# A four-layer image network on one core: a convolution folded with the projection before it, and a normalisation on another engine

## The chip, the cores and the metric

The kernel runs on one core of a Trainium2 chip. A core has a matrix engine (TensorE, PE in the profile; its weight loads are listed apart as PEld), three engines for elementwise work (VectorE or DVE, ScalarE or ACT, GpSimd or POOL) and SyncE (SP), whose queue issues all the DMAs of this kernel. The engines run side by side, each in the order of its own queue. The metric is the device time of one execution in microseconds.

## The reference

The input is two images of 96 channels and 96 x 96 pixels, in float32. Each of four layers adds to its input a block that works on the group-normalised input: x = x + layer(gn(x)). All four blocks hold selective scans, recurrences h = a * h + b over 192 channels with 16 states each. Layer 0, the only one whose work changes, begins like this (`_gn` has 32 groups of three channels and no weights):

```python
xz = in_proj(gn(x))                # 96 -> 384 channels; the halves are xp and z
t  = conv3x3(xp, off1_w) + off1_b  # 192 -> 192 channels, zero padding
t  = gelu(batch_norm(t))
f  = tanh(off2(t))                 # 192 -> 2 channels: an offset for each pixel
xs = xp sampled bilinearly at the places that f gives
```

The sampled `xs` is then scanned in windows of 6 x 6 pixels in four directions. The four results are added, normalised over the channels, multiplied with silu(z) and projected back to 96 channels.

## The kernel before

Layer 0 is the class `Windows`, on a `Machine` whose tiles are T = 288 pixels wide. The layers 1, 2 and 3 run after it on a second machine (T = 384) as one common stretch, the trunk.

*Strips, jobs and steps.* Layer 0 cuts the two images into 32 strips of six rows (576 pixels). A strip has eight jobs: four directions by two halves of 288 pixels. A job has eight steps, and each step scans a group of channels and states as 128 partitions by 864 values. So a strip is 64 steps, and the layer 2048. `Machine.scan` walks over the steps n and writes out, in this order, what each engine gets at step n:

- PE: every second step `four_B` (into the tile `pb`, one for two steps), and `sum_states` of step n-2 (six products of the trace, into `py`).
- ACT: `decay` for step n+1, three activations into `dA`, and then whatever was put in the slot with `self.act` in the step before.
- DVE: the product `pd` of the loaded `w` with `pb`, and the scan `hs` of `dA` and `pd`.
- What the generators in flight have for this step: the next job's preamble (the products `wx` and `dtw`, the copy `p`, the two activations `v`, softplus), and the background jobs in `bg`.
- POOL: `hC`, the product of `hs` with the loaded `C`, which `sum_states` reads two steps later.

*The order is set by the program.* The class `Engine` chains all the instructions of an engine in the order in which the program issues them. It also issues them on one line of the file, which is why nearly every row of the profile names L156. Rows are told apart by their tiles.

*Sampling a strip.* `samples` is the generator that prepares the next strip while the present one is scanned. A `yield` ends what it does in a step. It starts with the preamble of a strip's first job, which runs ten steps ahead, so at step 6 of job 6 of the strip before:

1. It loads eight rows of the input (the strip and a row above and below) into `x8`, and on DVE `apply_gn` subtracts the group's mean and multiplies by its inverse deviation: the group `x<-x,gn`.
2. `in_proj`, four products with `w_in`, copied by ACT into `xp`, which has two halves of 96 channels, eight rows and 98 columns. The columns at the sides stay zero.
3. The convolution: for each half of the output channels and each half of the strip, 18 products (two halves of the input by nine taps) add up in a bank of PSUM, `po`. Four or three stand in each step, so it spans 20 steps. ACT copies each `po` with scale and bias of the batch norm into `t`.
4. Gelu on `t`, four pairs of products with `off2`, tanh into `f`, then some 18 products and sums on POOL that sample `xp` (tiles `top` and `t`).

*Ending a strip.* When a strip's last job is done, `ending` runs as a background generator beside the first jobs of the next strip: `channel_norm` on `yn` (products with a matrix of means into `pm` and `pb`, Ln and Exp on ACT), the normalisation of the strip's own input on DVE (`xn<-x,gn`), the projection of `z` in four products, silu, `w_out`, and the residual sum `o` on DVE. The method `bank` keeps apart the users of the only PSUM bank `pm`: in `Windows`, steps 7, 0 and 1 of a job belong to the preamble.

*Functions that share an ACT table.* An `ACT_TABLE_LOAD` stands in ACT's queue wherever the next function needs other tables: around softplus, gelu, silu, and for Ln and Exp.

*Weights.* `pack` brings the weights into the shapes of the loads, on the host. Before the change, `off1` is one load of 96 x 2 x 9 x 192 values.

Of the kernel before, what the change touches and what calls it, by code (L numbers as in the profile page):

```python
# [33 lines left out]
F32 = mybir.dt.float32  # L34
AF = mybir.ActivationFunctionType
ALU = mybir.AluOpType
# [4 lines left out]
B, C, S, L = 2, 96, 96, 96 * 96  # L41
# [34 lines left out]
def pack(i):  # L76
    i = {k: np.asarray(v) for k, v in i.items()}
    a = {"x": i["x"].reshape(B, C, L)}

    sel = np.zeros((32 + N, 4, 32, 4), np.float32)  # L80
    for q in range(4):
        for n in range(4):
            sel[32 + 4 * q + n, q, :, n] = 1
    a["sel"] = sel.reshape(32 + N, 512)
    a["zs"] = np.repeat(np.eye(32, dtype=np.float32), 4, 0)
    eye = np.eye(96, dtype=np.float32)
    gn = np.kron(np.eye(32), np.ones((3, 3))).astype(np.float32) / np.float32(3)
    one = np.ones((96, 96), np.float32)
    a["mats"] = np.stack([gn, one / np.float32(96), one / np.float32(192), eye, eye[::-1]], 1)

    q = lambda n: i[f"L0_conv_{n}"]
    a["L0_in"] = q("in_proj_w").T
    a["L0_out"] = _lhsT(q("out_proj_w"))
    off = q("off1_w").transpose(1, 2, 3, 0).reshape(2, 96, 9, 192)
    a["L0_off1"] = off.transpose(1, 0, 2, 3)
    off2 = _lhsT(q("off2_w").reshape(2, 192))
    a["L0_off2"] = np.broadcast_to(off2[..., None], (96, 2, 2, 96))
    a["L0_cols"] = _cols(
        q("off1_b"), q("bn_gamma"), q("bn_beta"), q("bn_mean"), q("bn_var"), q("ln_gamma"), q("ln_beta")
    )  # L100
    a |= _scan_weights(
        "L0", q("x_proj_weight"), q("dt_projs_weight"), q("dt_projs_bias"),
        q("A_logs").reshape(4, 192, N), q("Ds").reshape(4, 192),
    )

    q = lambda n: i[f"L1_conv_{n}"]
    a["L1_in"] = q("in_proj_w").T
    a["L1_out"] = _lhsT(q("out_proj_w"))


    w, taps = q("in_proj_w").T[:, :192], q("conv_w").reshape(192, 4)
    a["L1_in3"] = np.stack([np.concatenate([w, w[32 * t : 32 * t + 32]]) for t in range(3)], 1)
    a["L1_taps"] = np.repeat(np.stack([taps[:, :3].T, np.stack([taps[:, 3]] * 3)]), (96, 32), axis=0)
    a["L1_cols"] = _cols(q("conv_b"))
    a["L1_norm"] = np.stack([q("norm_g"), q("norm_b")], 1)
    a["L1_g1"] = q("gate_w1").T
    a["L1_g1b"] = q("gate_b1").reshape(24, 1)
    a["L1_g2"] = q("gate_w2").T
    a["L1_g2b"] = q("gate_b2").reshape(1, 4)
    a |= _scan_weights(  # L120
        "L1", q("x_proj_w")[None], q("dt_proj_w")[None], q("dt_proj_b")[None], q("A_log")[None], q("D")[None]
    )

    q = lambda n: i[f"L2_conv_{n}"]
    a["L2_in"] = q("in_proj_w").T
    a["L2_out"] = _lhsT(q("out_proj_w"))
    a["L2_taps"] = np.broadcast_to(q("conv_w").reshape(192, 9).T, (96, 9, 192))
    a["L2_cols"] = _cols(q("conv_b"), q("gn_gamma"), q("gn_beta"))
    a |= _scan_weights(
        "L2", q("x_proj_w"), q("dt_w"), q("dt_b"), q("A_logs").reshape(4, 192, N), q("Ds").reshape(4, 192)  # L130
    )

    q = lambda n: i[f"L3_conv_{n}"]
    a["L3_in"] = q("in_proj_w")
    a["L3_out"] = _lhsT(q("out_proj_w").T)
    a["L3_taps"] = np.broadcast_to(q("conv_w").reshape(192, 9).T, (96, 9, 192))
    a["L3_cols"] = _cols(q("conv_b"), q("ln_gamma"), q("ln_beta"))
    a |= _scan_weights(
        "L3", q("x_proj_weight").transpose(0, 2, 1), q("dt_proj_weight"), q("dt_proj_bias"),
        q("A_log")[None], q("D_skip")[None],  # L140
    )
    return {k: np.ascontiguousarray(v) for k, v in a.items()}
# [396 lines left out]
class Layer:  # L539
# [81 lines left out]
        return (yield from self.averaged(mv, self.const["gn"], 1e-5, f"gn{self.n}"))  # L621

    def apply_gn(self, out, x, gn):
        self.nc.vector.tensor_scalar(out, x, gn[:, 0:1], gn[:, 1:2], ALU.subtract, ALU.mult)

    def channel_norm(self, x, mat, sq):

# [22 lines left out]
    def ending(self, y, src, dst, stats, sz=None, xn=None, norm=None, gamma=None, beta=None):  # L650


        nc, hs = self.nc, range(2)
        size = y.shape[-1]
        sb = lambda tag, *shape, bufs=1: self.sb.tile([96, *shape], F32, tag=tag, name=tag, bufs=bufs)
        if sz is None:
            x, n = sb("x", size, bufs=3), sb("xn", size, bufs=3)
            nc.sync.dma_start(x, src)
            yield
        if norm is not None:  # L660
            yield from self.channel_norm(y, norm, sb("sq", 2, size))
        if sz is None:
            xn(n, x)
        else:
            x, z = sb("x", size, bufs=2), sb("z", 2, size, bufs=2)
            nc.sync.dma_start(z, sz)
            nc.sync.dma_start(x, src)
        if gamma is not None:
            for h in hs:
                self.act(  # L670
                    lambda h=h: nc.scalar.activation(
                        y[:, h, :], y[:, h, :], AF.Identity, scale=gamma(h), bias=beta(h)
                    )
                )
        yield
        if sz is None:
            z = sb("z", 2, size)
            for h in hs:
                for at in self.pieces(size):
                    yield from self.bank()  # L680
                    m = self.mm(self.ps()[:, : self.T], [(self.w_in[:, 192 + 96 * h : 288 + 96 * h], n[:, at])])
                    self.act(lambda h=h, at=at, m=m: nc.scalar.copy(z[:, h, at], m))
                    yield
            self.act(lambda: nc.scalar.activation(z, z, AF.Silu))
            yield
        yield
        for h in hs:
            nc.gpsimd.tensor_mul(y[:, h, :], y[:, h, :], z[:, h, :])
            yield
        o = sb("o", size, bufs=2)  # L690
        for i, at in enumerate(self.pieces(size)):
            yield from self.bank(2)
            m = self.mm(self.ps()[:, : self.T], [(self.w_out[:, h, :], y[:, h, at]) for h in hs])
            yield
            nc.vector.tensor_add(o[:, at], x[:, at], m)
            if stats is not None:
                nc.vector.bn_stats(stats[:, i, :], o[:, at])
            yield
        nc.sync.dma_start(dst, o)


class Windows(Layer):
# [9 lines left out]
    def load_weights(self):  # L712
        super().load_weights()
        nc = self.nc
        self.off1, self.off2 = self.load("off1"), self.load("off2")

        self.bn = self.w.tile([96, 2, 2], F32, tag="bn", name="bn")
        v = lambda i: self.cols[:, 2 * i : 2 * i + 2]
        s, b = self.bn[:, 0, :], self.bn[:, 1, :]
# [6 lines left out]
    def samples(self, st):  # L726
        nc, b, s = self.nc, st["b"], st["s"]
        gn = self.gns[b]
        lo, hi = max(6 * s - 1, 0), min(6 * s + 7, S)
        o = lo - (6 * s - 1)  # L730
        x = self.sb.tile([96, 8 * S], F32, tag="x8", name="x8", bufs=1)
        nc.sync.dma_start(x[:, o * S : (o + hi - lo) * S], self.src[b, :, lo * S : hi * S])
        yield
        if o:
            nc.gpsimd.memset(x[:, :S], 0.0)
        if o + hi - lo < 8:
            nc.gpsimd.memset(x[:, (o + hi - lo) * S :], 0.0)
        self.apply_gn(x[:, o * S : (o + hi - lo) * S], x[:, o * S : (o + hi - lo) * S], gn)
        yield

        xp = self.xp
        for h in range(2):
            for i in range(2):
                yield from self.bank()
                p = self.mm(
                    self.ps()[:, :384], [(self.w_in[:, 96 * h : 96 * h + 96], x[:, 384 * i : 384 * i + 384])]
                )
                o = xp[:, h, 4 * i : 4 * i + 4, 1:97]
                self.act(lambda o=o, p=p: nc.scalar.copy(o, p.rearrange("p (r c) -> p r c", c=S)))
# [3 lines left out]
        for h in range(2):  # L753
            for i in range(2):
                p = self.ps(pool=self.po, tag="po")
                for n in range(18):
                    hk, tap = divmod(n, 9)
                    dy, dx = divmod(tap, 3)
                    nc.tensor.matmul(
                        p[:, :288], self.off1[:, hk, tap, 96 * h : 96 * h + 96],  # L760
                        xp[:, hk, dy + 3 * i : dy + 3 * i + 3, dx : dx + S], start=n == 0, stop=n == 17,
                    )
                    if n in (3, 7, 11, 14):
                        yield
                self.act(
                    lambda h=h, i=i, p=p: nc.scalar.activation(
# [52 lines left out]
    def run(self, src, dst, stats_in, stats_out):  # L819
# [2 lines left out]
        self.gns = [at_once(self.group_norm(stats_in[:, b])) for b in range(B)]  # L822
        self.m.persistent()
        self.xp = self.sb.tile([96, 2, 8, 98], F32, tag="xp", name="xp", bufs=1)
        for h in range(2):
            nc.gpsimd.memset(self.xp[:, h, :, 0:98:97], 0.0)
        jobs, strips = [], [{"b": b, "s": s} for b in range(B) for s in range(16)]
# [73 lines left out]
class Cross(Layer):  # L901
# [174 lines left out]
    def stage_conv(self, im):  # L1076
# [52 lines left out]
        yield  # L1129
        yield  # L1130
        for c in range(self.nch):
            self.act(lambda x=x: nc.scalar.activation(x, x, AF.Identity, scale=gn[:, 1:2], bias=gn[:, 2:3]))
            yield
            x6 = xps[c % 2]
            if c + 1 < self.nch:
# [36 lines left out]
class Gated(Cross):  # L1172
# [18 lines left out]
    def stage(self, im):  # L1191
# [12 lines left out]
        def chunk(c):  # L1204
# [2 lines left out]
            nc.sync.dma_start(xn, self.src[b, :, at])  # L1207
            yield
            yield
            self.act(lambda: nc.scalar.activation(xn, xn, AF.Identity, scale=gn[:, 1:2], bias=gn[:, 2:3]))  # L1210
            yield
            yield
            yield from self.channel_norm(xn.unsqueeze(1), self.const["m96"], self.t1("sq1", 2).unsqueeze(1))
# [253 lines left out]
```

## Time and profile before

| | |
|---|---|
| time, median of 9 runs | 29034.89 us (29003.41 to 29093.88) |
| the profiled execution | 29093.88 us, the slowest of the nine |
| its span, first to last instruction | 29092.1 us |
| first scan of layer 0; last | 157.1 us; 7603.4 us |
| busy, whole span | PE 76%, PEld 24%, DVE 86%, ACT 65%, POOL 65% |
| granted TensorE clock, whole span | 0.646 |
| granted TensorE clock, 375.5 to 7389.9 us | 0.66 |
| `po` products | 4608, 1421.0 us busy |
| `hC` on POOL; `hs` on DVE; `pd` on DVE | 15591.8; 15825.3; 8464.6 us busy |

A row of the costliest groups gives line, engine, operation, the tile written and the tiles read, shape, count, then busy us, mean ns of one instruction, idle us of the engine just before them and what ended most of it. A row of the waits reads "who waited <- for whom: us in total, times, longest us". In the 40 slices a digit is the busy share in tenths, and for PEclk the granted clock in tenths. Matrix products are pipelined, so the mean ns of one is longer than the distance from one start to the next. The timeline gives start, length, engine, line and operation, with equal neighbours merged.

### The profile page before, as it was taken

How to read it: one execution, taken by the hardware profiler on the slowest of the kernel's cores; microseconds unless marked ns; L12 is line 12 of the kernel's file. 1: busy time of each engine (PE TensorE's matmuls, PEld its weight loads, DVE VectorE, ACT ScalarE, POOL GpSimd, SP SyncE). 2: the span in 40 equal slices, each digit the busy share in tenths (PEclk: the TensorE clock that was granted, in tenths of full speed). 3: DMA queues.
4: the chain of work that ended last, by engine and by line, in shares of the span. 5: the costliest groups of instructions: out<-in, count | busy, mean ns of one | idle time of the engine just before them, and what ended most of it. 6: DMA issues, size and time to landing. Idle time of an engine off the chain costs nothing. (4 is left out here: it accounts for less than half of the span.)

```text
span 29092.1 us, 269563 instructions
## 1 busy us (share of the span) xinstructions
PE 22213.7 (76%) x72312; PEld 6982.8 (24%) x72312; DVE 25156.3 (86%) x15459; ACT 18934.5 (65%) x40441; POOL 18838.7 (65%) x9508
## 2 busy tenths in 40 slices
PE   7888888887567777777778777777777778776777
PEld 2222233332112222222222221212222122221112
DVE  7888888888457778877889999999999989999999
ACT  5666666666567676676666776567765666665566
POOL 5777777767346566665666666666666656666667
PEclk7666666666566667777776675556765577655556
DMA  3333333333344445444444544454444544444444
GB/s 97 101 100 100 101 102 101 98 98 101 66 100 128 125 126 148 144 134 133 136 145 150 145 144 135 142 158 144 145 142 143 156 141 141 146 139 135 133 135 141
DMA packets 3285863, 3707.11 MB, mean 127 GB/s; under 512 B 756928, under 2 KB 3260518, under 8 KB 3284232
## 3 DMA queue, kind: packets, MB, share of 16 engines
q1 hardware_dynamic: 3284328, 3689.86, 42.8%
q8 instruction: 570, 9.34, 0.1%
q14 instruction: 965, 7.91, 0.1%
HBM read 2933.04 MB, written 755.57 MB: 127 GB/s over the span
## 5 line engine op out<-in xcount | busy, mean ns | idle before, releaser
L156 POOL TENSOR_TENSOR hC<-hs,C 128x1152 f32<-128x1152 f32 (+1 forms) x6656 | 15591.8, 2343 | 8610.1 <-PE py L156 4132.5
L156 DVE TENSOR_TENSOR_SCAN hs<-dA,pd 128x1158 f32<-128x1158 f32 (+1 forms) x6656 | 15825.3, 2378 | 1060.1 <-ACT hc L156 119.9
L156 ACT ACTIVATE dA<-d,w_alog 128x384 f32<-128x384 f32 (+1 forms) x19968 | 10305.9, 580 | 6627.0 <-DVE hs L156 5703.6
L156 DVE TENSOR_TENSOR pd<-w,pb 128x1158 f32<-128x1158 f32 (+1 forms) x6656 | 8464.6, 1272 | 1684.7 <-PE pb L156 583.3
L156 PE MATMUL py<-hC,zs 128*32 128x384 f32 (+1 forms) x39936 | 7790.6, 677 | 2760.9 <-POOL hC L156 2659.1
L156 PE MATMUL pb<-p,sel 16*128 16x386 f32 (+1 forms) x6656 | 4155.5, 716 | 487.6 <-ACT cz L156 168.9
L156 ACT ACT_TABLE_LOAD x2837 | 3639.9, 1283 | 108.6 <-DMA w_alog<-in_L_alog 44.4
L156 PE MATMUL pm<-p,w_dtw 6*96 6x384 f32 (+1 forms) x3328 | 2250.2, 772 | 1703.0 <-ACT p L156 973.5
L156 PEld LDWEIGHTS py<-hC,zs 128*32 128x32 f32 x39936 | 1213.8, 129 | 7913.7 <-POOL hC L156 4918.6
L156 PE MATMUL pm<-x,w_in 128*96 128x384 f32 (+1 forms) x2554 | 1540.5, 759 | 984.0 <-ACT p L156 799.5
L156 PEld LDWEIGHTS pb<-p,sel 16*128 16x128 f32 x6656 | 1362.2, 254 | 2680.1 <-issue 987.6
L156 PE MATMUL pm<-x,w_taps 96*96 96x384 f32 x3456 | 1510.5, 581 | 38.6 <-ACT xs L156 20.2
L156 PE MATMUL po<-xp,w_off 96*96 96x288 f32 x4608 | 1421.0, 454 | 26.7 <-ACT t L156 24.8
L156 PE MATMUL pm<-xs,w_wx 96*80 96x384 f32 x2304 | 1394.3, 750 | 52.8 <-DMA xs<-flatc 20.1
L156 PEld LDWEIGHTS pm<-p,w_dtw 6*96 6x96 f32 x3328 | 590.5, 231 | 3326.5 <-ACT p L156 1476.9
L156 ACT COPY w<-hc 128x6 f32<-128x6 f32 x4416 | 831.4, 194 | 505.4 <-DMA w<-du 459.4
L156 ACT ACTIVATE v<-pm,w_scol 96x384 f32<-96x384 f32 (+1 forms) x1664 | 909.6, 547 | 226.1 <-PE pm L156 163.4
L156 POOL TENSOR_TENSOR du<-v,xs 96x768 f32<-96x768 f32 x576 | 1044.3, 1813 | 8.8 <-ACT v L156 8.8
L156 PEld LDWEIGHTS pm<-x,w_in 128*96 128x96 f32 (+1 forms) x2554 | 570.2, 246 | 1973.5 <-ACT p L156 989.2
L156 PEld LDWEIGHTS po<-xp,w_off 96*96 96x96 f32 x4608 | 781.9, 179 | 644.8 <-issue 323.4
L156 PEld LDWEIGHTS pm<-x,w_taps 96*96 96x96 f32 x3456 | 610.7, 192 | 936.2 <-issue 720.0
L156 ACT COPY hc<-hs 128x3 f32<-128x3 f32 x4608 | 830.5, 180 | 5.7 <-DVE hs L156 5.7
(213 smaller groups left out, 13151.8 us busy)
## 6 DMA issues: line engine op xcount, KB each, us to landing
d<-delta SPq DMA_DIRECT2D x3456, 192.0 KB, 3.4
w<-du SPq DMA_DIRECT2D x3456, 192.0 KB, 3.5
C<-C SPq DMA_DIRECT2D x2304, 192.0 KB, 3.4
d<-delta SPq DMA_DIRECT2D x1536, 144.0 KB, 2.7
w<-du SPq DMA_DIRECT2D x1536, 144.0 KB, 2.6
delta<-v SPq DMA_DIRECT2D x576, 288.0 KB, 2.7
du<-du SPq DMA_DIRECT2D x576, 288.0 KB, 3.4
C<-C SPq DMA_DIRECT2D x1024, 144.0 KB, 2.7
```

Source lines behind the costliest of these rows:

```text
L156: r = traced(*args, **kwargs)
```

## The change

Two linear maps in a row, in_proj and the convolution of the offsets, become one convolution of the normed input. The kernel computes its weights at the start: for each of the nine taps, the transposed in_proj weights (2 x 96 x 96) times the tap's weights (2 x 96 x 192), as two products that add up to 96 x 192, copied by ACT into `off1`. The convolution then runs over the 96 channels of `x` instead of the 192 of `xp`: nine products a bank instead of 18, at the same 20 steps. `in_proj` into `xp` stays, since the sampling reads it. For its taps `x` gets the form that `xp` has, eight rows of 98 columns with zero sides, in a tile `x8` that lasts through the layer; the load writes its inner 96 columns.

`apply_gn` becomes an activation on ACT, scale times x plus bias, with the bias that `averaged` already made. It is called through `self.act`, so it stands in the slot of the step after. In `samples` one more step is left before it and two behind it; the in-projection stays at the step where it was. In `ending` one `yield` is added, so that the projection of `z` and what follows it up to silu move one step later. The layers 1 to 3 used the same activation before; they now call the common method.

```diff
     a["L0_in"] = q("in_proj_w").T
-    off = q("off1_w").transpose(1, 2, 3, 0).reshape(2, 96, 9, 192)
-    a["L0_off1"] = off.transpose(1, 0, 2, 3)
+    a["L0_inT"] = q("in_proj_w")[:192].reshape(2, 96, 96).transpose(1, 0, 2)
+    off = q("off1_w").transpose(2, 3, 1, 0).reshape(9, 2, 96, 192)
+    a["L0_off1"] = off.transpose(0, 2, 1, 3)
...
     def apply_gn(self, out, x, gn):
-        self.nc.vector.tensor_scalar(out, x, gn[:, 0:1], gn[:, 1:2], ALU.subtract, ALU.mult)
+        self.nc.scalar.activation(out, x, AF.Identity, scale=gn[:, 1:2], bias=gn[:, 2:3])
...
         if sz is None:
-            xn(n, x)
+            self.act(lambda: xn(n, x))
...
         if sz is None:
             z = sb("z", 2, size)
+            yield
             for h in hs:
...
-        self.off1, self.off2 = self.load("off1"), self.load("off2")
+        self.off2 = self.load("off2")
+
+        inT = self.load("inT")
+        self.off1 = self.w.tile([96, 9, 192], F32, tag="off1", name="off1")
+        for tap in range(9):
+            t = self.sb.tile([96, 2, 192], F32, tag="off", name="off")
+            nc.sync.dma_start(t, self.A["L0_off1"][tap])
+            p = self.mm(self.ps()[:, :192], [(inT[:, h, :], t[:, h, :]) for h in range(2)])
+            nc.scalar.copy(self.off1[:, tap, :], p)
...
-        x = self.sb.tile([96, 8 * S], F32, tag="x8", name="x8", bufs=1)
-        nc.sync.dma_start(x[:, o * S : (o + hi - lo) * S], self.src[b, :, lo * S : hi * S])
-        yield
+        x = self.x8
         if o:
-            nc.gpsimd.memset(x[:, :S], 0.0)
+            nc.gpsimd.memset(x[:, :1, :], 0.0)
         if o + hi - lo < 8:
-            nc.gpsimd.memset(x[:, (o + hi - lo) * S :], 0.0)
-        self.apply_gn(x[:, o * S : (o + hi - lo) * S], x[:, o * S : (o + hi - lo) * S], gn)
+            nc.gpsimd.memset(x[:, 7:, :], 0.0)
+        inner = x[:, o : o + hi - lo, 1:97]
+        nc.sync.dma_start(inner, self.src[b, :, lo * S : hi * S].rearrange("p (r c) -> p r c", c=S))
+        yield
+        yield
+        self.act(lambda: self.apply_gn(inner, inner, gn))
+        yield
         yield
...
-                for n in range(18):
-                    hk, tap = divmod(n, 9)
+                for tap in range(9):
                     dy, dx = divmod(tap, 3)
                     nc.tensor.matmul(
-                        p[:, :288], self.off1[:, hk, tap, 96 * h : 96 * h + 96],
-                        xp[:, hk, dy + 3 * i : dy + 3 * i + 3, dx : dx + S], start=n == 0, stop=n == 17,
+                        p[:, :288], self.off1[:, tap, 96 * h : 96 * h + 96],
+                        x[:, dy + 3 * i : dy + 3 * i + 3, dx : dx + S], start=tap == 0, stop=tap == 8,
                     )
-                    if n in (3, 7, 11, 14):
+                    if tap in (1, 3, 5, 7):
                         yield
```

In the order of instructions the change takes 64 elementwise instructions from DVE (28 of 96x768, 4 of 96x672, 32 of 96x576) and gives ACT as many, and 9 copies at the start. PE loses half of the `po` products and gets 18 at the start. SP issues nine loads more.

## The prediction

> **What bounds the kernel now.** I read the page first, for the stages and their costliest groups; then the table by stretch; then the waits of DVE; then single stretches of the timeline. Layer 0 fills the first ten and a half of the 40 slices; the change touches nothing after it.
>
> ```profile
> DVE  7888888888457778877889999999999989999999
> PEclk7666666666566667777776675556765577655556
> L156 DVE TENSOR_TENSOR_SCAN hs<-dA,pd 128x1158 f32<-128x1158 f32 (+1 forms) x6656 | 15825.3, 2378 | 1060.1 <-ACT hc L156 119.9
> L156 PE MATMUL po<-xp,w_off 96*96 96x288 f32 x4608 | 1421.0, 454 | 26.7 <-ACT t L156 24.8
> ```
>
> DVE is the fullest engine, in layer 0 at eight tenths. It makes one product `pd` and one scan `hs` per step. Counting scans (64 a strip) puts the first scan of strip 0 at 157.1 us, of strip 1 at 375.5 and of strip 31 at 7389.9. Strips 1 to 30 therefore take 7014.4 / 30 = 233.8 us each. Strip 31 samples nothing, because no strip follows it. From here "step 1.3" means job 1, step 3 of a strip. The table by stretch has strips 1 to 30, then the two parts of strip 18 (its convolution, its rest), then strip 31; columns are length, busy us of PE, PEld, DVE, ACT and POOL, granted clock, DMA share, GB/s:
>
> ```profile
> 375.50:7389.90 7014.40, 5681.64 (x21362) 2113.75 (x21360) 6108.90 (x4559) 4399.99 (x8277) 5026.82 (x2824) 0.66 0.34 100
> 4338.60:4415.00 76.40, 71.85 (x330) 34.81 (x331) 64.22 (x49) 50.43 (x95) 46.40 (x26) 0.97 0.30 85
> 4415.00:4568.40 153.40, 114.43 (x386) 34.22 (x381) 139.64 (x105) 96.69 (x183) 120.84 (x70) 0.51 0.37 111
> 7389.90:7606.70 216.80, 148.15 (x526) 42.76 (x526) 201.60 (x151) 127.35 (x245) 143.67 (x76) 0.53 0.32 96
> ```
>
> Strip 31 is nature's experiment: the same scans and the same ending of the strip before, no sampling, 216.8 us. Sampling costs a strip 17.0 us although all of it but one operation runs beside DVE. The waits of DVE say how; first strips 1 to 30, then strip 31:
>
> ```profile
> DVE pd L156 <- PE pb L156: 250.9, 62, 8.9
> DVE y L156 <- PE py L156: 90.9, 98, 1.6
> DVE yn L156 <- PE py L156: 90.5, 58, 3.9
> DVE hs L156 <- ACT dA L156: 75.9, 63, 1.4
> DVE x L156 <- DMA x<-in_x: 41.9, 29, 3.1
> ...
> DVE yn L156 <- PE pm L156: 19.1, 7, 3.2
> ```
>
> ```profile
> DVE y L156 <- PE py L156: 1.5, 1, 1.5
> DVE pd L156 <- PE pb L156: 1.2, 1, 1.2
> DVE hs L156 <- ACT dA L156: 1.1, 2, 0.6
> DVE yn L156 <- PE py L156: 0.3, 1, 0.3
> ```
>
> The first list is 599 us with the lines left out, 20.0 a strip; the second is 4.1. The difference, 15.9, and the 1.1 us of the group norm itself account for the 17.0. PE is most of it: 451.4 / 30 = 15.0 a strip against 3.0.
>
> **Part 1, half the convolution.** Every product of the program stands twice in the trace (4608 `po` = 32 strips x 144). The change leaves 72 a strip, in the same 20 steps (7.7 to 2.2), as the order of instructions shows. Their pitch, from two stretches of PE's timeline, at half clock and at full:
>
> ```profile
> 5735.46 4.05 PE L156 MATMUL po<-xp,w_off 96*96 96x288 f32 x8
> 5739.43 1.18 PE L156 MATMUL py<-hC,zs 128*32 128x288 f32 x6
> 5740.55 1.27 PE L156 MATMUL pm<-p,w_dtw 6*96 6x288 f32 x2
> ...
> 4359.76 2.18 PE L156 MATMUL po<-xp,w_off 96*96 96x288 f32 x8
> 4361.87 0.69 PE L156 MATMUL py<-hC,zs 128*32 128x288 f32 x6
> ```
>
> Eight `po` take 3.97 us to the next start at half clock (0.50 each) and 2.11 at full (0.26); a step's six `py` take 1.12 and 0.62 (to 4362.49). The same stretches give 1.25 and 0.68 for a pair of `pb`, 2.0 and 1.0 for the four products of `wx`, 1.2 and 0.65 for two of `dtw`. PE's work per job of 8 steps during the convolution, at half clock, after the change: `po` 28.8 x 0.50 = 14.3; `py` 8 x 1.12 = 9.0; `pb` 4 x 1.25 = 5.0; `wx` 2.0; `dtw` 2.4; the ending's 24 products spread over the 20 steps, 9.6 x 0.50 = 4.8. That is 37.5 us; at full clock it is 19.8. Before it is 51.8 and 27.0. DVE needs 26.5 for an undisturbed job (pitches of 3.18 and 3.25, and two of 3.62 where a job ends). So before, PE is the slower one even at full clock; after, it is faster at full clock and still slower at half. The convolution is 2.5 jobs, 66 us of DVE.
>
> Of the 12.0 us of PE waits above strip 31's, 1.8 belong to part 3; 10.2 are the convolution's: about 3.2 where it begins and 6 at step 1.3. If the clock is full for part of it, PE keeps up so long as the half-clock share f satisfies f x 26.5/37.5 + (1-f) x 26.5/19.8 >= 1, that is f up to 0.54. The trace says activity decides the clock (0.97 with the convolution, 0.51 and 0.53 without), and the change halves the largest part of that activity, so I do not count on 0.97. I take half of the waits as gone: 5.1 us a strip; the bounds are 10.2 and 0 (a loss is rival 1).
>
> [...]
>
> **Part 2, group norm off DVE.** This is the group that goes, and the row of the same ScalarE form in layer 2's staging:
>
> ```profile
> L156 DVE TENSOR_SCALAR x<-x,gn 96x768 f32<-96x768 f32 x28 | 31.3, 1118 | 52.7 <-DMA x<-in_x 52.7
> L156 ACT ACTIVATE x<-x,gn 96x576 f32<-96x576 f32 x88 | 75.2, 854 | 0.0
> ```
>
> The strip's own normalisation stands at step 6.7 and holds DVE for 1.1 us and for the load, 41.9 / 30 = 1.4 us; the pitch there is 5.68 against 3.24, so 2.4 go. The second one (96x576, 565 ns) adds 0.47 to its pitch. Together 2.9 us a strip, nearly sure. On ACT, 96x480 takes 782 ns and 96x576 854, so 96x768 is an estimate of 1.0. It lands at step 7.1, after the first `v`, and the in-projection's first product at 7.2 waits for it; behind it in ACT's queue stands softplus with its two table loads of 1.28. The load has one step more than before to arrive, with rows of 384 B instead of one run; its issue passes nothing else on SP. The other takes 0.85 at step 1.5, ahead of the two `yn` activations. ACT waits for DVE 1467 us in the 6000 us from 1000 on, so it has room on average, not after three table loads at 1.2. Bounds 0 and the full 1.85 a strip; I take 0.4, since an ordinary softplus step, 3.7 us beside 1.4 of `dA`, is covered now.
>
> [...]
>
> **Part 3, the ending is one step later.** Gelu (step 2.4) and Silu of `z` (2.5) stood in neighbouring steps, each 1.16 between two table loads; DVE lost 1.8 there to `pb` and 1.4 of `dA` more than strip 31. Silu now stands at 2.6, behind the first `f`, which frees PE's bank. The waits shrink or move: 0 to 3.2; I take 1.2.
>
> **Start.** The first convolution is four times 36 `po` in 8.97 us, alone: half of it, 18 us, goes. Nine weight loads through two buffers, each pair some 2.7 (a 216 KB load of x lands in that) + 1 of products, add about 17, and ACT's copies stand ahead of the group norm. Net 0, within 8.
>
> **Sum.** 2.9 + 5.1 + 1.2 - 0.4 = 8.8 a strip, x 30 = 264; strip 0, whose waits are 7.8 in all, perhaps 5; strip 31 0.5. That is 270 us: 29,094 - 270 = 28,824 for the profiled execution, which was the slowest of the nine (span 29,092 and 2 around it). Against their median of 29,035 it makes 28,765.
>
> **Rivals.** (1) The clock stays at half through the convolution. Then PE needs 37.5 against 26.5: 11.0 x 2.5 = 27, less about 3 that a step's lead covers, 24 instead of 10.2. With parts 2 and 3 that is 10.1 a strip lost: 29,350. It decides from f = 0.86: there 66 us of work take 83, which less the lead of 3 leaves 13.9 of waits, and 3.7 more than now eat parts 2 and 3. For it: less activity, and 0.5 in every stretch without convolution. Against: a saturated PE at half clock got the full one in every strip that convolves. 9%. (2) The clock stays near full and the convolution's waits vanish: 13.9 x 31 = 431, 28,604. For it: strip 0, where nothing but the convolution stands beside the scans, waits only 4.2 for PE. 25%. (3) ACT takes back 4 us a strip at 1.2 to 1.5 and 7.1 to 7.3: 28,890. 15%. (4) The waits of 1.3 follow from the table loads, not from PE's load, and parts 2 and 3 are all but eaten by ACT: within 0.2% of 29,035. 6%. The forecast has 45%.
>
> **Range.** All bounds at their best (16.3 x 31) give about 28,520, at their worst about 29,010. I give 28,560 to 28,950: it leaves out rival 1, most of rival 4 and the extremes, under 2 in 10. 0.2% (58 us) is about what a measurement here can tell. Faster: the forecast and rivals 2 and 3, 85%; same 6%; slower 9%.
>
> **What would show it.** Right: no `x<-x,gn` on DVE; `po` at 2304; strips of about 225; DVE's waits on `pb` and `yn <- PE py` in strips 1 to 30 near half of 250.9 and 90.5; the convolution's clock between 0.6 and 0.9. Wrong: waits on `pb` as long as before (clock near 0.5), DVE's wait on `dA` well over 75.9, or the span after 7606 us, which holds trunk layers alone, changed by more than its noise.

## The result, and the profile after

The changed kernel is slower: 29189.78 us (median of 9 runs, 29168.99 to 29202.01) against 29029.13 for the kernel before (29 runs), a ratio of 1.0053 with a 95% interval of 1.0044 to 1.0061. The forecast was 28,765.

From the page of the changed kernel, the DVE and PEclk rows of the 40 slices and two of the costliest groups:

```profile
DVE  7888888888547788887899999999999989999999
PEclk6555555555566667777776675556765577655556
L157 PE MATMUL po<-x,off 96*96 96x288 f32 x2304 | 1174.8, 654 | 6.5 <-ACT t L157 6.5
L157 DVE TENSOR_TENSOR_SCAN hs<-dA,pd 128x1158 f32<-128x1158 f32 (+1 forms) x6656 | 15825.3, 2378 | 1008.9 <-ACT hc L157 114.7
```

The count of `po` is half, as the diff says. But its products take 654 ns each instead of 454, and the granted clock reads 5 where it read 6 in the slices of layer 0. The table by stretch, with the rows that the prediction showed (strips 1 to 30; 76 us of strip 18's convolution and the rest of that strip; strip 31) and the trunk behind them; columns as before:

```profile
380.40:7534.20 7153.80, 6119.15 (x19202) 2040.81 (x19200) 6078.43 (x4501) 4453.84 (x8336) 5019.54 (x2824) 0.53 0.33 98
4428.00:4504.00 76.00, 72.80 (x216) 28.09 (x214) 54.35 (x41) 42.74 (x80) 39.15 (x22) 0.57 0.27 80
4504.00:4666.90 162.90, 133.08 (x427) 40.43 (x427) 148.31 (x110) 106.00 (x199) 128.13 (x74) 0.50 0.36 107
7534.20:7751.00 216.80, 150.79 (x528) 43.34 (x526) 201.18 (x150) 127.91 (x246) 144.05 (x76) 0.51 0.32 96
7751.00:29174.00 21423.00, 16083.55 (x49558) 4713.12 (x49558) 18615.71 (x10542) 14240.15 (x31613) 13478.49 (x6481) 0.64 0.46 138
```

A strip takes 7153.8 / 30 = 238.5 us, 4.6 more than the 233.8 before. The clock of strip 18's convolution is 0.57 where it was 0.97; over the first 76 us of strips 1 to 30 it is 0.57 after and 0.91 before. PE is busy 72.8 of 76 us all the same: it has 216 products instead of 330, and one takes 72.8 / 216 = 0.34 us instead of 71.85 / 330 = 0.22. Strip 31, without sampling, takes 213.5 us from its first scan to its last before and 212.8 after.

From its first scan to its last, layer 0 takes 7590.7 us against 7446.4: 144 more, most of the 161 by which the medians differ (5.6 of it in strip 0). The trunk from the last scan of layer 0 to the last scan took 21399 us here, 21461 in the profile before, and 21480 to 21532 in most of the kernels below, though none of them touches it. The runs also fell on several chips, where the kernel before took 29029 to 29161 us. So below, layer 0 from first to last scan is compared. Now the waits of DVE in strips 1 to 30:

```profile
DVE pd L157 <- PE pb L157: 343.5, 211, 5.8
DVE y L157 <- PE py L157: 221.8, 119, 3.8
DVE yn L157 <- PE pm L157: 78.1, 56, 1.6
DVE yn L157 <- PE py L157: 76.0, 56, 2.0
DVE hs L157 <- POOL hC L157: 25.8, 109, 0.5
DVE hs L157 <- ACT dA L157: 21.6, 36, 0.6
```

The four PE rows are 719.4 us, 24.0 a strip against 15.0. The wait on `dA` fell from 75.9 to 21.6 us (-1.8 a strip), the wait for the load of x is gone (-1.4), and so are the two group norms on DVE (-1.1 and -0.6). 9.0 - 1.8 - 1.4 - 1.1 - 0.6 = 4.1 of the 4.6. Parts 2 and 3 did what they were for, and PE took back more than all of it.

### The profile page after: what moved, and what is told of

Its sections match the earlier page's. It is cut to its first block, busy times and chain, and to the rows that moved or that the text cites. A ratio compares the mean times of both kernels' runs of the same rounds, so it can differ in the third digit from the quotient of the medians.

```text
span 29174.8 us, 264983 instructions
## 1 busy us (share of the span) xinstructions
PE 22601.2 (77%) x70044; PEld 6890.1 (24%) x70044; DVE 25122.5 (86%) x15395; ACT 18994.2 (65%) x40514; POOL 18830.5 (65%) x9509
## 5 line engine op out<-in xcount | busy, mean ns | idle before, releaser
L157 PE MATMUL py<-hC,zs 128*32 128x384 f32 (+1 forms) x39936 | 8060.6, 699 | 2731.3 <-POOL hC L157 2629.9
L157 PE MATMUL pb<-p,sel 16*128 16x386 f32 (+1 forms) x6656 | 4321.0, 743 | 484.6 <-ACT cz L157 171.3
L157 PEld LDWEIGHTS pb<-p,sel 16*128 16x128 f32 x6656 | 1421.7, 265 | 2784.8 <-issue 1130.0
L157 PE MATMUL po<-x,off 96*96 96x288 f32 x2304 | 1174.8, 654 | 6.5 <-ACT t L157 6.5
L157 PE MATMUL py<-xs,diag 96*96 96x384 f32 x1152 | 803.8, 795 | 0.0
```

Source lines behind the costliest of these rows:

```text
L157: r = traced(*args, **kwargs)
```

## The experiments

### Each half of the change alone

The question was which part loses. The first kernel has the folded convolution, with the group norms on DVE at their old steps:

```diff
 def apply_gn(self, out, x, gn):
-    self.nc.scalar.activation(out, x, AF.Identity, scale=gn[:, 1:2], bias=gn[:, 2:3])
+    self.nc.vector.tensor_scalar(out, x, gn[:, 0:1], gn[:, 1:2], ALU.subtract, ALU.mult)
...
-        yield
-        self.act(lambda: self.apply_gn(inner, inner, gn))
-        yield
+        self.apply_gn(inner, inner, gn)
...
```

The ending has its old steps again (in the part of the edit left out here), and layers 1 to 3 keep their activation.

> Part 1 alone: the folded convolution, but both group norms on VectorE and the ending at its old steps. Clock theory (half the products no longer earn the full TensorE clock, so PE at half rate falls behind DVE): the convolution's stretch is granted 0.5 to 0.6 as in the changed kernel (0.56), and without parts 2 and 3 a strip is about 4 us longer than the changed kernel's 238.9, 242 to 244; time 29,260 to 29,330 us. Rival (the added activations on ScalarE cause the loss): strips under 233.8, time under 29,035.

The second starts from the kernel before, with its 18 products a bank, and makes parts 2 and 3 alone:

```diff
 def apply_gn(self, out, x, gn):
-    self.nc.vector.tensor_scalar(out, x, gn[:, 0:1], gn[:, 1:2], ALU.subtract, ALU.mult)
+    self.nc.scalar.activation(out, x, AF.Identity, scale=gn[:, 1:2], bias=gn[:, 2:3])
...
-            xn(n, x)
+            self.act(lambda: xn(n, x))
...
             z = sb("z", 2, size)
+            yield
...
```

> Parts 2 and 3 alone: group norm on ScalarE and the ending one step later, the convolution with 18 products a bank as before. Clock theory: the convolution keeps a clock of 0.9 or more, and a strip loses 2.4 us at step 6.7, 0.4 for the second norm and about 1.5 at Gelu and Silu: 229 to 230.5 instead of 233.8, time 28,900 to 28,940 us, faster than before by 0.3 to 0.5%. Rival (ScalarE): strips of 236 or more, slower than before.

Measured: part 1 alone 29061.97 us, 0.9965 [0.9951, 0.9979] of the kernel before; parts 2 and 3 alone 28989.49, 0.9937 [0.9925, 0.995]. Strips of 230.1 and 228.3 us, so 3.7 and 5.5 gained a strip. Together they lose 4.6. That is the surprise of the case, and it was not what I expected of the first kernel: neither part loses, only the two together do. Strips of 230.1 us are where the rival (ScalarE) had put the first kernel, not the 242 to 244 of the clock theory; the second kernel's 228.3, against the rival's 236 or more, and the sections below speak against that rival. The two longest waits of DVE for PE, first with part 1 alone, then with parts 2 and 3 alone (strips 1 to 30):

```profile
DVE pd L157 <- PE pb L157: 235.3, 100, 5.8
DVE y L157 <- PE py L157: 73.7, 79, 3.8
```

```profile
DVE pd L156 <- PE pb L156: 219.3, 62, 8.1
DVE y L156 <- PE py L156: 100.6, 118, 1.6
```

All waits for PE together are 11.8 and 13.1 us a strip, where they were 15.0 before the change and 24.0 after it. The clock of the first 76 us, mean over the strips, is 0.76 with part 1 alone and 0.93 with parts 2 and 3. The same nine-tap convolution got 0.76 in one kernel and 0.57 in the other. PE has the identical list of products where the convolution begins. Here is PE's timeline there, of the changed kernel and then of part 1 alone:

```profile
4424.37 1.18 PE L157 MATMUL py<-hC,zs 128*32 128x288 f32 x6
4425.48 2.21 PE L157 MATMUL pm<-xr,w_wx 96*80 96x288 f32 x4
4427.48 2.13 PE L157 MATMUL po<-x,off 96*96 96x288 f32 x4
4429.54 1.18 PE L157 MATMUL py<-hC,zs 128*32 128x288 f32 x6
4430.65 1.27 PE L157 MATMUL pm<-p,w_dtw 6*96 6x288 f32 x2
```

```profile
3153.26 1.18 PE L157 MATMUL py<-hC,zs 128*32 128x288 f32 x6
3154.37 2.21 PE L157 MATMUL pm<-xr,w_wx 96*80 96x288 f32 x4
3156.38 1.34 PE L157 MATMUL po<-x,off 96*96 96x288 f32 x4
3157.65 0.69 PE L157 MATMUL py<-hC,zs 128*32 128x288 f32 x6
3158.27 0.72 PE L157 MATMUL pm<-p,w_dtw 6*96 6x288 f32 x2
```

The two run in step (1.11 us from `py` to `wx`, 2.0 to `po`) until, in the second, the clock rises in the middle of the four `po`: the next `py` take 0.69 instead of 1.18. The records of the granted clock show where it changes. From 400 to 7000 us the kernel before has 164 stretches at one clock, 0.5 or 1.0, and the changed kernel 68, and each of them lasts a whole multiple of 3.413 us, to within a nanosecond. A stretch of 3.413 us is called a window below, and the times at which windows meet are the edges of a grid. In the second kernel an edge fell at 3156.8, 2.4 us after the start of `wx`, and the clock rose there; in the first one fell at 4428.5, 3.1 us after it, and the clock stayed at half. The windows before and after those edges, first of the changed kernel, then of part 1 alone (busy times of PE, PEld, DVE, ACT and POOL, then the granted clock):

```profile
4425.12:4428.54 3.42, 3.42 (x10) 1.80 (x8) 3.20 (x3) 0.39 (x1) 2.25 (x2) 0.50 0.31 86
4428.54:4431.95 3.41, 3.41 (x12) 0.88 (x10) 2.61 (x3) 1.37 (x3) 1.48 (x2) 0.50 0.43 114
```

```profile
3153.38:3156.79 3.41, 3.41 (x11) 1.50 (x12) 3.19 (x3) 0.80 (x3) 2.24 (x2) 0.50 0.47 131
3156.79:3160.21 3.42, 3.42 (x17) 1.44 (x16) 3.29 (x4) 1.52 (x5) 2.20 (x2) 1.00 0.37 112
```

PE is busy to the last hundredth in the first window of both; only one of them is followed by full clock. Busy time alone does not tell them apart. The second one holds more of `py` (1.0 us against 0.4), whose products contract over 128 rows, where those of `po` and `wx` contract over 96.

### One tap instead of nine

One rival was that ACT, with a group norm and a later silu more in its queue, had become the limit. This kernel leaves out eight of the nine taps, so its convolution is a 1x1 map, and keeps everything else:

```diff
                 for tap in range(9):
-                    nc.tensor.matmul(..., start=tap == 0, stop=tap == 8)
+                    if tap == 4:
+                        nc.tensor.matmul(..., start=True, stop=True)
```

> The changed kernel with only the middle one of the nine taps: it leaves out eight ninths of the convolution's products, so its output is another. PE's demand at half clock falls from 37.5 to about 25 us a job, under DVE's 26.5. Clock theory: the clock stays at 0.5 and it does not matter; waits of DVE for PE fall from 24 us a strip to about 5, a strip takes 219 to 223 us. Rival (ScalarE or the order of the steps holds DVE): strips stay over 232.

Measured in a single run: 28689.28 us beside 29158.52; strips of 220.1 us. Its row for the convolution of a middle strip, then its longest waits:

```profile
4097.30:4173.30 76.00, 61.55 (x190) 19.23 (x190) 68.68 (x51) 55.74 (x102) 49.85 (x27) 0.53 0.33 96
```

```profile
DVE pd L157 <- PE pb L157: 88.5, 75, 1.5
DVE y L157 <- PE py L157: 77.2, 60, 1.6
DVE hs L157 <- ACT dA L157: 43.2, 51, 1.4
```

With the clock as low as in the changed kernel, the waits for PE fall from 24.0 to (88.5 + 77.2) / 30 = 5.5 us a strip when PE's demand goes. ACT had all its new work and held DVE for 1.4 a strip. The loss is PE's work at half clock, and ACT is not the limit. Rival 4, waits that come from the table loads and stay without PE's load, falls too: the table loads are all still there.

### Rows, columns or busy time

If the clock follows how much of the array is in use, the convolution can be given more of the array without one product more. This kernel adds 32 rows to each of its products, ones in the input times zeros in the weights:

```diff
-        self.x8 = self.sb.tile([96, 8, 98], F32, ...)
+        self.x8 = self.sb.tile([128, 8, 98], F32, ...)
+        nc.gpsimd.memset(self.x8[96:], 1.0)
...
-        self.off1 = self.w.tile([96, 9, 192], F32, ...)
+        self.off1 = self.w.tile([128, 9, 192], F32, ...)
+        nc.gpsimd.memset(self.off1[96:], 0.0)
...
```

> The changed kernel with the same number of products, but each contracts over 128 rows instead of 96: the 32 rows added hold ones in the moving operand and zeros in the weights, so they add nothing. A product takes no longer. If the clock is granted by how much of the array is in use (my reading of the two traces: a window at half clock is followed by a full one when products fill about a quarter of the array-time), a product counts 4/3 as much, the clock of the convolution rises to 0.8 or more, waits on PE fall to under 10 us a strip, a strip takes 221 to 228, time 28,650 to 28,880 us. If only the time counts in which PE is busy, nothing changes: strips of 238.9, time near 29,190.

The quarter of the array-time in this expectation was my estimate from the two windows above; no run shows such a point. Measured: 28834.61 us, 0.9884 [0.9869, 0.9899] of the kernel before on the same chip; strips of 223.9 us; the clock of the first 76 us 0.84 over the strips. A convolution of this kernel by stretch, the row of `po` in its groups, its waits:

```profile
4174.60:4250.60 76.00, 59.85 (x261) 24.97 (x260) 67.45 (x51) 54.25 (x100) 49.58 (x27) 0.88 0.31 94
```

```profile
L157 PE MATMUL po<-x,off 128*96 128x288 f32 x2304 | 843.4, 493 | 149.1 <-ACT t L157 149.1
```

```profile
DVE pd L157 <- PE pb L157: 165.7, 98, 4.2
DVE y L157 <- PE py L157: 108.0, 62, 3.2
```

The same 2304 products take 843 us instead of 1175. PE is busy 60 of 76 us instead of 73, and the waits for PE are (165.7 + 108.0) / 30 = 9.1 a strip instead of 24.0. No work was taken from any engine, and ACT has all its new work here too. Two `po` in a row start 0.48 us apart at half clock and 0.24 at full in both kernels; the clock is what differs. Three kernels tell rows from columns and from data. One widens the weights to 128 output columns, with the 32 extra columns a copy that nobody reads; one has both; one has the 32 rows with zeros in the input too (its line is shown against the kernel with 128 rows):

```diff
-                        p[:, :288], self.off1[:, tap, 96 * h : 96 * h + 96],
+                        p[:, :288], self.off1[:, tap, 96 * h : 96 * h + 128],
...
```

> The changed kernel with convolution products of 128 output columns instead of 96; the 32 more repeat other columns of the weights and are not read. If the clock goes by array use, rows or columns alike, the convolution's clock is 0.8 or more and a strip takes 221 to 229; the weights' load is a third longer, which may lengthen the pitch of a product by up to 0.08 us and cost up to 2 us of that. If only rows in use count (the run with 128 rows), strips stay at 235 to 239.

> Both: convolution products of 128 rows and 128 columns, 1.78 times the array use of the changed kernel's. By array use the clock of the convolution is over 0.9, waits on PE are under 5 us a strip above those of a strip without sampling, a strip takes 219 to 224 us, time 0.7 to 1.6% under the kernel before. If 128 rows alone gave all there is to get (223.9), no shorter, and the longer weight loads make it 224 to 227.

```diff
-        nc.gpsimd.memset(self.x8[96:], 1.0)
+        nc.gpsimd.memset(self.x8[96:], 0.0)
```

> The run with 128 rows, with zeros instead of ones in the 32 added rows of the moving operand, whose weights are zero too. If the clock goes by the rows that an instruction names, nothing changes: convolution's clock about 0.84, strips of about 223.9. If it goes by what the rows carry, the clock is that of the changed kernel, 0.57, and strips are 235 to 239.

| kernel | rows x columns of `po` | layer 0, us | strip, us | clock of its first 76 us | time, and the kernel before beside it |
|---|---|---|---|---|---|
| changed | 96 x 96 | 7590.7 | 238.5 | 0.57 | 1.0053 [1.0044, 1.0061] |
| columns | 96 x 128 | 7582.6 | 238.3 | 0.59 | 29304.0, 29161.24 (single run) |
| rows | 128 x 96 | 7142.4 | 223.9 | 0.84 | 0.9884 [0.9869, 0.9899] |
| rows and columns | 128 x 128 | 7129.7 | 223.4 | 0.85 | 0.988 [0.9863, 0.9896] |
| rows of zeros | 128 x 96 | 7139.6 | 223.8 | 0.84 | 28843.19, 29093.51 (single run) |

Among these five kernels rows count (a clock of 0.84 and 0.85 with 128, 0.57 and 0.59 with 96), columns don't, and it makes no difference whether the added rows of the input carry ones or zeros (0.84 with either; their weights are zero in both). The kernel with both was to get a clock over 0.9 by array use; it got 0.85, as with the rows alone. A convolution of the kernel with 128 columns, by stretch:

```profile
4434.70:4510.70 76.00, 71.63 (x216) 30.28 (x214) 54.03 (x41) 42.48 (x80) 39.27 (x22) 0.59 0.28 80
```

It reads like the changed kernel's. The distance from one `po` to the next stayed at 0.48 us at half clock, so it is not a longer product that hides a gain of the columns. The load of 128 columns took 222 ns on average against 191 for 96 (both over 128 rows), 16% more where a third was expected.

Among these kernels the clock of the convolution went with the rows of its products. But part 1 alone got 0.76 with 96 rows, and at what point the clock rises, no run shows. In the changed kernel the window from 4425.12 us, with PE busy for 3.42 us of it, is followed by half clock, and the one from 4455.84, with PE busy for 3.42 us too, by full clock. Nor does the full clock last there. After it rises at 4459.3, PE is busy for 3.41, 3.41 and, when it has caught up, 2.12 us of the next three windows, and the one after them is at half again. From 400 to 7000 us the 34 stretches at full clock of the changed kernel last two to five windows, 21 of them three (10.2 us). With 18 taps there was enough left to do for longer ones: of the 82 in the kernel before, 49 last 34.1 or 37.5 us.

### A delay on another engine

If the loss depends on where the edges of the grid fall, a little idle work on DVE, which lengthens a strip, should change it, and perhaps for the better. The edits add one, two, or (once, in the step of strip 2 alone) three operations on a tile that nobody reads:

```diff
         nc.sync.dma_start(inner, self.src[b, :, lo * S : hi * S].rearrange("p (r c) -> p r c", c=S))
         yield
+        for _ in range(1):
+            nc.vector.tensor_scalar(self.idle, self.idle, 1.0, None, ALU.mult)
         yield
...
```

> The changed kernel with one more operation on DVE at step 6.7, where the group norm stood: a 96x768 multiplication by one of a tile that nobody uses, 0.7 to 1.1 us of pure extra work in every strip. Theory of the phase (PE issues the same products at the same pitch at a convolution's start in the changed kernel and with the folded convolution alone; the clock differs only because the fixed 3.41 us windows fall otherwise on them): the extra work shifts the pattern against the windows and a strip may get shorter, 226 to 236 us instead of 238.9, and its length lies near a whole number of windows (66 to 69 of them). Theory of plain activity (too little work for the full clock wherever the windows fall): 239 to 240, one more window at most 242.3.

> As the run with one idle DVE operation a strip, with two of them, 1.4 to 2.2 us of extra work, about what the group norm and its load held DVE before. Theory of the phase: again a length near a whole number of windows, as likely 228.7 or 232.1 as 238.9; with this much extra the changed kernel is nearest to the folded convolution alone (228.7 in most strips). Plain activity: 240 to 242.3.

> The changed kernel with three idle 96x768 operations on DVE at step 6.7 of strip 2 alone, 2 to 3.3 us once in the layer. Theory of a lock on the windows: strip 2 gets longer, the phase is another for a few strips (some of 226 to 235 us), and then the pattern falls back to 238.9 as it does in the changed kernel after strips 6 and 12; the layer from first to last scan takes 7,570 to 7,600 us (7,590.7). If any phase could last, most strips after it stay at another length, under 236, and the layer takes 7,350 to 7,520.

Single runs: with one idle operation a strip, 29152.77 us beside 29161.24, layer 0 in 7451.1; with two, 29095.03, layer 0 in 7427.1. More work on the engine that bounds the layer makes it 140 and 164 us shorter than the changed kernel's 7590.7. The operation and a convolution of the first of them:

```profile
L157 DVE TENSOR_SCALAR idle<-idle x32: 529/530/595, 78.5 to 7137.6; 96x768 f32<-96x768 f32 x32
```

```profile
3185.50:3261.50 76.00, 70.21 (x233) 27.96 (x232) 58.55 (x45) 45.30 (x86) 42.53 (x23) 0.66 0.28 80
```

Half a microsecond more on DVE, and the clock goes from 0.57 to 0.66 (0.63 over the strips). With two operations 30 of the 64 took about 2.25 us, so the work added is nearer 2.8 us a strip; its strips vary between 226.1 and 241.6 us, and the forecast of a length near a whole number of windows did not hold for most of them. Two operations bring back 164 of the 251 us between the changed kernel and part 1 alone (7340.1); what makes the rest was not tried. Many strip lengths lie near whole multiples of the 3.413 us. In the changed kernel 27 of the strips 1 to 30 take 238.6 to 239.3 us, and 70 windows are 238.93. In the kernel before the usual strip is 232.1 to 232.4 (68 windows, 232.1), with part 1 alone 228.7 (67 windows, 228.7). With one idle operation lengths mostly alternate between about 232.0 and 235.6, near 68 and 69 windows (232.1 and 235.5); a pair is 467.6, and 137 windows are 467.6. A strip of a whole number of windows meets the grid at the same place again, and in the changed kernel 20 of the 34 stretches at half clock are 67 windows long. That the same products go without the full clock every time for that reason is my reading; it was not shown. With the single push strip 2 takes 233.3 and the next 238.9; up to strip 13 a few strips of 231.8 to 235.5 follow, and from strip 14 on all take 238.6 to 239.3. The layer finds its way back, and with 7573.4 us the push gains almost nothing (29214.73 us beside 29093.51). Strips of the three kernels with 128 rows vary between 221 and 226 and keep to no one length.

## Why the prediction was wrong

**Step that failed: the clock in part 1.** "If the clock is full for part of it, PE keeps up so long as ... f up to 0.54", and "I take half of the waits as gone: 5.1 us a strip". The share of half clock came to about 0.86 (a mean of 0.57), and the waits for PE grew from 15.0 to 24.0 us a strip where 5.1 were to go. That is rival 1, but for three windows of full clock in most strips. The argument against it was that "a saturated PE at half clock got the full one in every strip that convolves". PE is saturated here too, and does not get it: I took PE's busy time as what the clock answers to; in the runs that changed the rows alone the clock followed them (0.57 with 96, 0.84 with 128, the same products otherwise). Strip 31, at 0.53 with PE busy for 148.15 of 216.80 us, had already spoken against busy time as the measure, and the argument left that out.

**Rival 1's sizes.** It was priced at 10.1 us a strip lost with half clock throughout, and break-even, 3.7 us more of waits, at f = 0.86; 4.6 were lost and the waits grew by 9.0. One likely reason why f = 0.86 cost more than priced stands in the trace, but no run tested it alone. The sum let PE use every full window whole. In fact PE has mostly caught up after two or three of them and stands idle in part of the last (1.3 of the 3.4 us from 4466.1 on, above), and the clock falls after it.

**Part 1 where the clock is given.** 128 rows against parts 2 and 3 alone: 228.3 - 223.9 = 4.4 us a strip, against 5.1. The half of the convolution was worth about what was forecast; its condition was not met.

**Part 2.** The pitch at step 6.7 went from 5.60 to 3.24 us, 2.4 as predicted. ScalarE's normalisation of 96x768 takes 1.017 us where 1.0 was estimated. It was to give back 0.4, and the waits for `dA` fell instead: rival 3 is out.

**Part 3.** The pitches of steps 2.6, 2.7 and 3.0 together fell by 1.57 us, against 1.2. Parts 2 and 3 alone gained 5.5 a strip where 2.9 + 1.2 - 0.4 = 3.7 stood; what makes the 1.8 more was not tried.

**Start and trunk.** The first scan comes at 156.3 us instead of 157.1, within the 0 ± 8. The trunk moved by less than it varies between kernels that leave it alone.

**The sum.** 8.8 us a strip was forecast; with the clock restored 10.0 came (233.8 to 223.9). The terms were nearly right, and adding them was the mistake: 3.7 and 5.5 make a loss of 4.6. My reading is that each part also moves PE's work against the grid of 3.413 us. The idle operations show that work of 0.5 to 2.8 us a strip on DVE alone moves the clock (0.57 to 0.63 over the strips with one of them), and the layer by 140 to 164 us; that this is the whole of the loss is not shown. The kernel with 128 rows is what the change was meant to be, and beats both the kernel before and the changed one.

## What to carry to other kernels

Taking work off PE slowed here what was left: with half the products the clock of the convolution fell from 0.91 to 0.57, and a product of that stretch took 0.34 us instead of 0.22. So cost PE's work at both clocks that the trace shows, and look at the granted clock of that stretch before and after. The convolution of the changed kernel had a clock of 0.57 with products over 96 rows, and 0.84 with the same products filled up to 128 rows with zeros, at 0.48 us from start to start at half clock with either, so the filling cost no time of its own. Where gains of two parts do not add (3.7 and 5.5 us a strip alone, a loss of 4.6 together), run each alone; a single measurement of a small change in such a kernel says little about the part that was changed.

## What the runs showed that was not expected

- In the records of the kernel before and of the changed one every stretch at one clock from 400 to 7000 us (164 and 68 of them) lasts a whole multiple of 3.413 us. Thirty-two rows of zeros in the convolution raised its mean clock from 0.57 to 0.84.
- Many strips take 67, 68 or 70 times 3.413 us, many in a row within 0.1 us, and come back to 70 after a push.
- 0.53 us more work a strip on the busiest engine made layer 0 140 us shorter (a single run).
- The idle operation, 96x768 on DVE from a tile of its own, takes 530 ns; the group norm of the same shape took 1118 in the kernel before. With two of them a strip 30 of the 64 took about 2250 ns. Why was not tried.
